# Layer 0's down projection: where the masked low-rank terms are multiplied

## The chip, the core and the metric

The kernel runs on one core of one Trainium2 chip. The core has TensorE (PE) for matrix products, VectorE (DVE), ScalarE (ACT) and GpSimd (POOL) for elementwise work, SyncE (SP) for issuing transfers, and 16 transfer (DMA) engines. PE writes its sums to PSUM, eight banks; the other operands lie in SBUF, on 128 partitions ("rows" below). The metric is device time in microseconds; the time before is the median of three runs, 1496.06 us (1492.9 to 1497.18).

## The reference, cut to what matters

Eight sequences of 128 tokens, 512 features, go through four layers. Each adds to `x` the result of an inner block followed by an outer one; everything is float32. The change touches the inner block of layer 0 only:

```python
# B = 8 sequences, H = 512, F = 1376, rank 16; an adapter per sequence
def lora_add(base, inp, A, B):
    Ab, Bb = A[0][lora_indices], B[0][lora_indices]
    t = einsum('bri,bni->bnr', Ab, inp)
    return base + einsum('bor,bnr->bno', Bb, t) * 0.5
gate = lora_add(einsum('bnh,fh->bnf', x, W_gate), x, A_gate, B_gate)
up   = lora_add(einsum('bnh,fh->bnf', x, W_up), x, A_up, B_up)
act  = silu(gate) * up
down = lora_add(einsum('bnf,hf->bnh', act, W_down), act, A_down, B_down)
```

So `down`, for each output feature and token, is a sum over 1376 hidden features plus a sum over 16 ranks of the sequence's own adapter. Layers 1 to 3 (adapters, an attention over a paged cache, experts) follow and are the same in both kernels.

## The kernel before, in words

Everything is kept transposed, features on the partitions and the 1024 tokens along the free dimension. The tokens are cut into four quarters of 256 (two sequences each); `quarter(j)` names the columns of quarter `j`, and `slot(j)` the partitions 32j to 32j+31. A half `g` is the quarters 2g and 2g+1.

**Low-rank terms.** `gathered` (L326) fetches with POOL the eight chosen adapters' rows: partition 32j+16i+r of `Bd` holds rank `r` of sequence 2j+i. So each slot has the two sequences of one quarter. `lora_down` (L574) multiplies `h` with the turned `Ad` into the PSUM tile `td`, one slot and one quarter at a time; `pair_masked` (L372) then halves it and sets to zero, in each slot, the ranks of the sequence that a token doesn't belong to. The result is `tdm`, 128 x 256: slot j, column t is for token t of quarter j.

**The hidden features.** 1376 is ten pieces of 128 and a last one of 96. `h` (128 x 11 x 1024) holds the activations; in its last piece the rows 96 to 127 are unused. The loop over pieces (`gates_by_seven`, L439) fills `h`. The weights `wd[k]` (`down_loaded`, L507) hold all 11 pieces for the output features 256k to 256k+255, loaded by SP while the gates run.

**The down projection.** `Down(g, k)` (L582) computes the 256 x 512 block of output half `k` and token half `g`, as 2 x 2 blocks of 128 x 256. The ten full pieces are cut into two halves of NH = 5 and multiplied by a Strassen-like scheme with seven block products in place of eight: `begin` does the first, `go_on` the other six. Sums of weights come from POOL (`down_weights`, L519), sums of activations from VectorE (`h_sums`, L532). At the end of `go_on` the last, 96-row piece is added to each of the four blocks by an ordinary product. Then `lora` (L621) adds the low-rank terms: for each block a product with only 32 rows, `Bd[slot(q)]` by `tdm[slot(q)]`, q the block's quarter. `out` (L626) evicts the four blocks to `y0`, one by ScalarE, three by VectorE, which also add what the scheme left in SBUF (`dp`, `du`).

**Order.** Instructions go to each engine's queue in the order in which the program lists them, and `kept` holds listed ones in place. Around the change TensorE does: the last gates (f = 10); the turning of `wb1`; `begin` of (0,0); `w11`; the turning of `Ad`; `begin` of (0,1); `td`; `go_on` of (0,0) and of (0,1); `lora` for both; (1,0) whole; the router products `midp` of half 0; (1,1) whole; `lora` for both; then layer 0's outer block (`midTp`, `eo`). SP's queue holds the gate weights, `wb1`, and behind them the loads of attention, which wait for room that the down projection frees. Several tiles share room by tag: `wb1` takes that of `Au`, the turned `Ad` that of `Bg`.

Of the kernel before, what the change touches and what calls it, by code (L numbers as in the profile page):

```python
# [10 lines left out]
F32 = mybir.dt.float32  # L11
# [6 lines left out]
P = 128  # L18
NB = 8
NT = NB * P  # L20
D = 512
DC = D // P
TG = NT // 512
FF = 1376
NF = (FF + P - 1) // P
# [22 lines left out]
def forward(ctx: ExitStack, tc: tile.TileContext, a: dict, out: bass.AP):  # L48
    nc = tc.nc
    pe, act, dve, pool, sp = nc.tensor, nc.scalar, nc.vector, nc.gpsimd, nc.sync  # L50
# [19 lines left out]
    w0 = c0.enter_context(tc.tile_pool(name="w0", bufs=1))  # L70
# [138 lines left out]
    def load_small(dst_pool, name, shape, src, tag=None, bufs=None):  # L209
        kw = {} if bufs is None else {"bufs": bufs}  # L210
        t = dst_pool.tile(shape, F32, tag=tag or name, name=name, **kw)
        sp.dma_start(t, src)
        return t
# [109 lines left out]
    with c0:  # L323
        psp = c0.enter_context(tc.tile_pool(name="psp", bufs=8, space=PSUM))

        def gathered(name, n):  # L326
            t = w0.tile([P, n], F32, tag=name, name=name)
            pool.indirect_dma_start(
                out=t, out_offset=None, in_=a[name],
                in_offset=bass.IndirectOffsetOnAxis(ap=row0_i[:, 0:1], axis=0),  # L330
            )
            return t
# [6 lines left out]
        Bg, Bu = gathered("Bg", FF), gathered("Bu", FF)  # L339
        Ad, Bd = gathered("Ad", FF), gathered("Bd", D)  # L340
# [19 lines left out]
        def quarter(j):  # L360
            return slice(j * NT // 4, (j + 1) * NT // 4)

        def slot(j):
            return slice(j * 32, (j + 1) * 32)

        def mmq(o, lhsT, rhs, start, stop):
            pe.matmul(o, lhsT, rhs, start=start, stop=stop, skip_group_check=True)  # L367

        def bank(name):
            return psp.tile([P, 2, NT // 4], F32, tag="mm", name=name)  # L370

        def pair_masked(dst, ps):  # L372

            dve.tensor_tensor(
                dst.rearrange("p (i t) -> p i t", i=2),
                ps.rearrange("p (i t) -> p i t", i=2),
                half2.unsqueeze(2).to_broadcast([P, 2, P]),
                ALU.mult,
            )
# [4 lines left out]
        tgm = w0.tile([P, NT // 4], F32, tag="tgm", name="tgm")  # L384
        tum = w0.tile([P, NT // 4], F32, tag="tum", name="tum")
# [11 lines left out]
        h = w0.tile([P, NF, NT], F32, tag="h", name="h")  # L397
# [103 lines left out]


        NH = NF // 2

        wd = []

        def down_loaded():  # L507
            for k in range(2):
                os_ = slice(2 * k * P, (2 * k + 2) * P)
                t = w0.tile([P, NF, 2 * P], F32, tag=f"wd{k}", name=f"wd_{k}")  # L510
                kept(sp.dma_start(
                    t[:, 0 : NF - 1, :],
                    a["WdT"][0 : (NF - 1) * P, os_].rearrange("(f p) o -> p f o", p=P),
                ))
                last = FF - (NF - 1) * P
                kept(sp.dma_start(t[:last, NF - 1, :], a["WdT"][(NF - 1) * P : FF, os_]))
                wd.append(t)

        def down_weights(k, t):  # L519
            w = wd[k]  # L520
            (a11, a12), (a21, a22) = (
                [w[:, NH * j : NH * (j + 1), i * P : (i + 1) * P] for j in range(2)] for i in range(2)
            )
            s1, s2, s4 = (t[:, n] for n in range(3))
            for o, l, r, op in (
                (s1, a21, a22, ALU.add), (s2, s1, a11, ALU.subtract),
                (a21, a11, a21, ALU.subtract), (s4, a12, s2, ALU.subtract),
            ):
                kept(pool.tensor_tensor(o, l, r, op))
            return a11, a12, a22, s1, s2, a21, s4  # L530

        def h_sums(g, t, held=lambda: None):  # L532
            (b11, b12), (b21, b22) = (
                [h[:, NH * i : NH * (i + 1), quarter(2 * g + j)] for j in range(2)] for i in range(2)
            )
# [6 lines left out]
        kept = tc.keep_in_program_order  # L542
# [8 lines left out]
        for f in range(1, NF):  # L551
            after = f + 1 < NF and weight_sums(f + 1, gate_weights(f + 1))
            gates_by_seven(f, A, itertools.islice(tabled, 15) if f < 3 else itertools.islice(angles, 3))
            A = after
            if f == 2:
                down_loaded()
            if f == NF // 2:
                AW = [down_weights(0, wop.tile([P, 3, NH, P], F32, tag="os", name="wds_0"))]
        cg.close()
        st = c0.enter_context(tc.tile_pool(name="st2", bufs=2, reuse_waits="tile"))  # L560


        wb1 = load_small(w0, "wb1", [P, D], a["wb1"], tag="Au")
        w11 = const.tile([P, 136], F32, tag="w11", name="w11")

        def ranks_to_ranks(wb1T):
# [5 lines left out]
        tdm = w0.tile([P, NT // 4], F32, tag="tdm", name="tdm")  # L572

        def lora_down(AdT):  # L574
            ps = bank("td")
            for f in range(NF):
                fw = min(P, FF - f * P)
                for j in range(4):
                    mmq(ps[slot(j), 0, :], AdT[:fw, f, slot(j)], h[:fw, f, quarter(j)], f == 0, f == NF - 1)
            pair_masked(tdm, ps[:, 0, :])  # L580

        class Down:  # L582

# [10 lines left out]
            def into(self, o, l, r, start=False):  # L594
                for f in range(NH):
                    mmq(o, l[:, f, :], r[:, f, :], start and f == 0, False)
# [6 lines left out]
            def go_on(self):  # L603
                a11, a12, a22, s1, s2, s3, s4 = AW[self.k]
                b11, b21, b22, t1, t2, t3, t4 = HB_[self.g]
                u, p1, even, odd = self.u, self.p1, self.even, self.odd
                self.into(odd[:, 1], s1, t1, True)
                self.into(odd[:, 0], s2, t2)
                kept(dve.tensor_tensor(u, odd[:, 0], p1, ALU.add))
                kept(dve.tensor_tensor(p1, odd[:, 1], p1, ALU.add))  # L610
                self.into(even[:, 1], s3, t3)
                kept(dve.tensor_tensor(p1, even[:, 1], p1, ALU.add))
                self.into(odd[:, 1], s4, b22)
                self.into(even[:, 0], a12, b21)
                self.into(even[:, 1], a22, t4)
                last = FF - 2 * NH * P
                for (i, j), ps in self.c.items():
                    mmq(ps, wd[self.k][:last, 2 * NH, i * P : (i + 1) * P],
                        h[:last, 2 * NH, quarter(2 * self.g + j)], False, False)

            def lora(self):  # L621
                for (i, j), ps in self.c.items():
                    o, q = 2 * self.k + i, 2 * self.g + j
                    mmq(ps, Bd[slot(q), o * P : (o + 1) * P], tdm[slot(q), :], False, True)

            def out(self):  # L626
                for (i, j), ps in self.c.items():
# [10 lines left out]
        downs = [Down(0, k) for k in range(2)]  # L638

        def meanwhile(blocks):  # L640
            HB_.append(blocks)
            wT = transposed(wb1, D, "wb1T", tag="AgT")
            downs[0].begin()
            ranks_to_ranks(wT)
            AW.append(down_weights(1, st.tile([P, 3, NH, P], F32, tag="wds", name="wds_1", bufs=1)))
            AT = transposed(Ad, FF, "AdT", tag="Bg")
            downs[1].begin()
            lora_down(AT)
# [4 lines left out]
        h_sums(1, st.tile([P, 3, NH, NT // 4], F32, tag="hs", name="hs_1", bufs=1), HB_.append)  # L653
        y0 = ypool.tile([P, DC, NT], F32, tag="y", name="y0")
        for d in downs:
            d.lora()
        for d in downs:
            d.out()
        turn_angles()
        downs = [Down(1, k) for k in range(2)]  # L660
# [4 lines left out]
        route0(0)  # L665
        downs[1].begin()
        downs[1].go_on()
        for d in downs:
            d.lora()
        for d in downs:  # L670
            d.out()

# [3 lines left out]
    with psa:  # L676
# [49 lines left out]
        kept = nc.dram_tensor("kept_x", (P, DC, NT), F32, kind="Internal").ap()  # L726
# [1607 lines left out]
```

## Time and profile before

| | |
|---|---|
| three runs: median (lowest, highest) | 1496.06 us (1492.9, 1497.18) |
| the profiled execution | 1490.35 us |
| its span, first to last instruction | 1488.6 us |
| TensorE clock granted | 0.999 of full speed |
| busy: PE, DVE, POOL, ACT | 1476.6, 1065.6, 856.4, 562.0 us |
| layer 0's down projection on the chain that ended last | 159.9 to 243.1 us, with `td` and the router |
| loads with `Bd` for `tdm`'s products | 32 records, at 201.37 and at 240.98 |

In the listings below, a row of the timeline is: start in us from the span's start, length in us, engine, line, operation, output<-inputs, rows*columns of the array (for PE), shape, count, and in brackets the idle time of that engine before it with what ended it. PEld is TensorE's loading of weights; it overlaps PE's products. A float32 product appears as two records. SPq is SP issuing a transfer.

### The profile page before, as it was taken

The numbers are of one execution on the slowest core, as the hardware profiler recorded it, in microseconds if no ns is written. First come the engines' busy times: TensorE is split into PE (matmuls) and PEld (weight loads), VectorE is DVE, ScalarE is ACT, GpSimd is POOL, SyncE is SP. The second block draws the span as 40 slices with busy tenths as digits, with TensorE's granted clock in tenths as the row PEclk, the third lists the DMA queues.
The fourth block names the chain that finished last, engine by engine and source line by source line (L and its number), as shares of the span: only waits on it lengthen the run. The fifth ranks groups of instructions, "written<-read, shape, count | busy, mean of one in ns | idle before, by whom it ended". The sixth has DMA issues, their size and how long they took to land.

```text
span 1488.6 us, 18093 instructions
## 1 busy us (share of the span) xinstructions
PE 1476.6 (99%) x5603; PEld 938.3 (63%) x5603; DVE 1065.6 (72%) x2121; ACT 562.0 (38%) x1422; POOL 856.4 (58%) x876
## 2 busy tenths in 40 slices
PE   9999999999999999999999999999999999999998
PEld 7888787455555655555555555565555555558887
DVE  4665425388888787787778778787878878855475
ACT  1111101044545544454554454454445455431110
POOL 2241104567777777776777777677777777622310
PEclk9999999999999999999999999999999999999999
DMA  7411001213545444564454455345445534433001
GB/s 242 118 44 32 1 1 55 94 36 115 183 148 173 150 119 129 150 183 126 135 152 131 128 158 177 110 135 163 129 125 166 168 106 138 120 104 98 1 9 52
DMA packets 155257, 171.44 MB, mean 115 GB/s; under 512 B 52624, under 2 KB 125776, under 8 KB 155024
## 3 DMA queue, kind: packets, MB, share of 16 engines
q1 hardware_dynamic: 136976, 133.18, 30.0%
q0 software_dynamic: 17056, 36.49, 7.7%
q8 instruction: 47, 0.77, 0.2%
q10 hardware_dynamic: 1120, 0.52, 0.1%
q14 instruction: 58, 0.48, 0.1%
HBM read 129.36 MB, written 40.76 MB: 114 GB/s over the span
## 4 chain that ended last, share of the span: by engine, by line
PE 96%; DVE 2%; ACT 0%; DMA 0%; issue 0%; DVEq 0%; ACTq 0%; SPq 0%
PE st L1173 18%; PE av L1225 18%; PE g L367 9%; PE q_six L979 8%; PE wo_two L979 6%; PE q_one L979 6%; PE q_five L979 6%; PE dn L367 5%; PE wo_six L979 4%; PE wo_one L979 4%; PE eo_l L53 3%; PE z L1761 2%; PE h L1761 2%; PE midp_l L53 1%; PE o L1761 1%; PE gu L367 1%
## 5 line engine op out<-in xcount | busy, mean ns | idle before, releaser
L922 POOL DMA_INDIRECT kn<-in_k_cache,kvrow_k x256 | 272.2, 1063 | 77.1 <-issue 71.2
L922 POOL DMA_INDIRECT vals<-in_v_cache,kvrow_v x256 | 272.3, 1064 | 73.6 <-issue 60.2
L1225 PE MATMUL av<-pT,vals 128*128 128x512 f32 x640 | 290.8, 592 | 0.2 <-DVE oT L1235 0.2
L1177 ACT ACTIVATE pT<-st,hide 128x512 f32<-128x512 f32 x256 | 175.9, 687 | 192.0 <-PE st L1173 178.8
L1173 PE MATMUL st<-qT,kT 128*128 128x512 f32 x512 | 237.4, 596 | 0.0
L1225 PEld LDWEIGHTS av<-pT,vals 128*128 128x128 f32 x640 | 121.4, 190 | 152.7 <-issue 148.3
L1078 POOL TENSOR_TENSOR vq<-q,txq 128x256 f32<-128x256 f32 x128 | 121.1, 976 | 130.6 <-ACT sqq L1052 92.9
L1173 PEld LDWEIGHTS st<-qT,kT 128*128 128x128 f32 x512 | 97.2, 191 | 109.3 <-issue 103.3
L1193 DVE TENSOR_TENSOR part<-pT 128x512 f32<-128x512 f32 x128 | 88.3, 691 | 76.2 <-ACT pT L1177 62.8
L979 PE MATMUL q_one<-q,x 128*128 128x384 f32 x256 | 93.0, 486 | 0.0
L1052 ACT ACTIVATE sqq<-q 128x128 f32<-128x128 f32 x252 | 78.2, 310 | 10.4 <-DVE q L1028 3.8
L979 PEld LDWEIGHTS q_one<-q,x 128*128 128x128 f32 x256 | 48.5, 190 | 39.8 <-issue 14.3
L979 PE MATMUL q_six<-q_s,xs_all 128*128 128x384 f32 x192 | 69.8, 486 | 0.0
L1033 ACT COPY q<-q_one 128x256 f32<-128x256 f32 x32 | 11.9, 372 | 151.9 <-PE q_one L979 133.5
L979 PE MATMUL wo_one<-o,oT 128*128 128x256 f32 x256 | 65.9, 380 | 1.1 <-ACT k L1033 0.8
L1173 PE MATMUL st<-qT,kTn 128*128 128x512 f32 x128 | 65.4, 592 | 0.0
L979 PE MATMUL wo_two<-o_s,os 128*128 128x256 f32 x256 | 60.6, 379 | 0.3 <-DVE os L938 0.3
L1177 ACT ACTIVATE pT<-st,rs 128x512 f32<-128x512 f32 x64 | 44.0, 687 | 38.5 <-PE av L1225 18.5
L979 PEld LDWEIGHTS wo_one<-o,oT 128*128 128x128 f32 x256 | 48.5, 190 | 15.0 <-issue 1.9
L436 POOL TENSOR_TENSOR ws<-wu 128x256 f32<-128x256 f32 (+1 forms) x9 | 6.4, 711 | 86.8 <-DMA wu<-in_WuT 79.8
L1209 ACT COPY rows<-rows 32x32 f32<-32x32 f32 x96 | 20.7, 216 | 92.1 <-DVE rows L1204 91.4
L367 PE MATMUL g<-xs,ws 128*128 128x256 f32 (+1 forms) x240 | 55.1, 379 | 0.0
(461 smaller groups left out, 2838.5 us busy)
## 6 DMA issues: line engine op xcount, KB each, us to landing
turned_new<-qkt SPq DMA_DIRECT2D x120, 160.0 KB
turned_cached<-kt SPq DMA_DIRECT2D x128, 128.0 KB
kT<-turned_cached SPq DMA_DIRECT2D x32, 512.0 KB
R<-sums SPq DMA_DIRECT2D x32, 512.0 KB
qT<-turned_new SPq DMA_DIRECT2D x30, 512.0 KB
q<-in_WqT SPq DMA_DIRECT2D x8, 1024.0 KB
o<-in_WoT SPq DMA_DIRECT2D x8, 1024.0 KB
kn<-in_k_cache,kvrow_k POOLq DMA_INDIRECT x256
```

Of the source, the lines that this page charges most:

```text
L53: pe.matmul(o, lhsT, rhs, start=start, stop=stop)
L367: pe.matmul(o, lhsT, rhs, start=start, stop=stop, skip_group_check=True)
L922: kept(pool.indirect_dma_start(out=d[:, c, :], out_offset=None, in_=kc if what == "k" else vc, in_offset=bass.IndirectOffsetOnAxis(ap=kvro ...
L979: kept(pe.matmul(o, l[:, c, :], r[:, c, :], start=start and c == 0, stop=c == 1, skip_group_check=True))
L1052: kept(act.activation(sq, S[n][m][:, j, i, :], AF.Square, accum_out=S[n]["ssq"][:, j, col : col + 1]))
L1078: kept(pool.tensor_tensor(to, t[:, b, :, hi : hi + 64], wx[:, b, lo : lo + 64].unsqueeze(2).to_broadcast(list(to.shape)), ALU.mult,))
L1173: kept(pe.matmul(ps, s["kT"][:, c, 4 * j : 4 * j + 4, :] if c < 4 else s["kn"][:, j], s["qT"][:, :, REP * j : REP * (j + 1), :].rearrange( ...
L1177: kept(act.activation(pT[:, c, :, :].rearrange("p i t -> p (i t)"), ps, AF.Exp, **(dict(bias=hide[:, b, c : c + 1]) if c < 4 else dict(bia ...
L1193: kept(dve.tensor_tensor(o, l, r, ALU.add))
L1209: kept(act.copy(rows[0:32, g, :], rows[32 * g : 32 * g + 32, 0, :]))
L1225: kept(pe.matmul(ps, v[:, c, :], pT[:, c, :, :].rearrange("p i t -> p (i t)"), start=c == 0, stop=c == NC - 1, skip_group_check=True,))
L1761: return pe.matmul(o, lhsT, rhs, start=start, stop=stop, skip_group_check=True)
```

## The change

The 32-row products of the low-rank terms are taken out (`lora` is gone). Instead the terms ride in the last piece's products, which have 128 rows now: the rows 96 to 127 of `h`'s last piece get `tdm`'s slot j in the columns of quarter j, by four ScalarE copies behind `pair_masked`; the weights' rows 96 to 127 get the rows of `Bd`. Since `Bd`'s rows differ from quarter to quarter, there must be four sets of last-piece weights. Quarter 0's lies in `wd` itself (`Bd`'s slot 0 is copied into it by two transfers when `wd` is loaded). Quarters 1, 2 and 3 have tiles of their own (`wl`), filled by eight transfers of SP (`last_loaded`): four bring the 96 rows of `W_down` once more from memory, four bring 32 rows of `Bd` from SBUF. Their tiles take the room of `Bu`, `tgm` and `tum`, which the last gate products are done with. The order of the other instructions on TensorE, VectorE and POOL is the same; on ScalarE the eviction of block (0,0) of `Down(1,0)` stands a few places earlier.

```diff
+        LAST = FF - (NF - 1) * P
-        wd = []
+        wd, wl = [], []
 ...
-                last = FF - (NF - 1) * P
-                kept(sp.dma_start(t[:last, NF - 1, :], a["WdT"][(NF - 1) * P : FF, os_]))
+                kept(sp.dma_start(t[:LAST, NF - 1, :], a["WdT"][(NF - 1) * P : FF, os_]))
+                kept(sp.dma_start(t[LAST:, NF - 1, :], Bd[slot(0), os_]))
                 wd.append(t)
+        def last_loaded():
+            wl.append([wd[k][:, NF - 1, :] for k in range(2)])
+            both = w0.tile([P, 2, D], F32, tag="Bu", name="wl_12")
+            ends = [w0.tile([P, 2 * P], F32, tag=t, name=f"wl_3_{t}") for t in ("tgm", "tum")]
+            wl.extend([[both[:, i, 2 * k * P : (2 * k + 2) * P] for k in range(2)] for i in range(2)])
+            wl.append(ends)
+            for t, h_ in ((both[:, 0], slice(0, D)), (both[:, 1], slice(0, D)), (ends[0], slice(0, 2 * P)), (ends[1], slice(2 * P, D))):
+                sp.dma_start(t[:LAST], a["WdT"][(NF - 1) * P : FF, h_])
+            for q, t, h_ in ((1, both[:, 0], slice(0, D)), (2, both[:, 1], slice(0, D)), (3, ends[0], slice(0, 2 * P)), (3, ends[1], slice(2 * P, D))):
+                sp.dma_start(t[LAST:], Bd[slot(q), h_])
 ...
         wb1 = load_small(w0, "wb1", [P, D], a["wb1"], tag="Au")
+        last_loaded()
 ...
             pair_masked(tdm, ps[:, 0, :])
+            for j in range(4):
+                act.copy(h[LAST:, NF - 1, quarter(j)], tdm[slot(j), :])
 ...
-                last = FF - 2 * NH * P
                 for (i, j), ps in self.c.items():
-                    mmq(ps, wd[self.k][:last, 2 * NH, i * P : (i + 1) * P],
-                        h[:last, 2 * NH, quarter(2 * self.g + j)], False, False)
-            def lora(self):
-                for (i, j), ps in self.c.items():
-                    o, q = 2 * self.k + i, 2 * self.g + j
-                    mmq(ps, Bd[slot(q), o * P : (o + 1) * P], tdm[slot(q), :], False, True)
+                    q = 2 * self.g + j
+                    mmq(ps, wl[q][self.k][:, i * P : (i + 1) * P], h[:, NF - 1, quarter(q)], False, True)
 ...
-        for d in downs:
-            d.lora()
         for d in downs:
             d.out()
```

The last removal stands twice, once for each half of the tokens.

More of the change, by code (lines that the diff above doesn't have):

```diff
@@ L667, in forward @@
         downs[1].go_on()
-        for d in downs:
-            d.lora()
         for d in downs:
```

## The prediction

> **What bounds the kernel now.** I read the page's head first: the busy shares, and the chain that ended last.
>
> ```profile
> PE 1476.6 (99%) x5603; PEld 938.3 (63%) x5603; DVE 1065.6 (72%) x2121; ACT 562.0 (38%) x1422; POOL 856.4 (58%) x876
> PE 96%; DVE 2%; ACT 0%; DMA 0%; issue 0%; DVEq 0%; ACTq 0%; SPq 0%
> ```
>
> TensorE is the bound over the whole span of 1488.6 us, and 96% of the chain is TensorE's own work. No other engine exceeds 72%. A busy PE is not proof of a bound, because a matmul's end is modelled; so I asked for the chain by pieces between 140 and 270 us, the end of layer 0's gates to the start of layer 1:
>
> ```profile
> 167.00 4.89 PE td L367 x88
> 171.89 48.62 PE dn L367 x230
> 220.51 3.71 PE midp_l L53 x32
> 224.22 18.87 PE dn L367 x94
> 243.08 0.59 PE midTp_l L288 x4
> 243.67 8.58 PE eo_l L53 x20
> ```
>
> Every piece begins where the last ends and all are PE. The down projection (`dn`) is therefore on the path that sets the end, and every PE microsecond taken out of it should move all that follows. Now the weight loads of TensorE over the two places where the diff removes products (start, length, what was loaded, count, idle before):
>
> ```profile
> 199.34 1.70 PEld L367 LDWEIGHTS dn<-h,wd 96*128 96x128 f32 x8
> 201.37 1.70 PEld L367 LDWEIGHTS dn<-tdm,Bd 32*128 32x128 f32 x16 [0.33 <-issue]
> 203.40 0.94 PEld L367 LDWEIGHTS dn<-h,wd 128*128 128x128 f32 x5 [0.33 <-PE dn L367]
> ...
> 218.40 1.70 PEld L367 LDWEIGHTS dn<-h,wd 96*128 96x128 f32 x8
> 220.13 0.99 PEld L53 LDWEIGHTS midp_l<-wmr,y 128*128 128x128 f32 x7
> ...
> 238.95 1.70 PEld L367 LDWEIGHTS dn<-h,wd 96*128 96x128 f32 x8
> 240.98 1.70 PEld L367 LDWEIGHTS dn<-tdm,Bd 32*128 32x128 f32 x16 [0.33 <-issue]
> 243.01 0.42 PEld L288 LDWEIGHTS midTp_l<-ident,mw_l 128*128 128x128 f32 x4 [0.33 <-PE dn L367]
> ```
>
> One f32 matmul shows as two records, so x16 are the eight low-rank products of one `lora` pass. The reader should see two things: each pass has a bubble of 0.33 us on either side, and at 218.40 the same 96-row piece is followed by full-array work 1.73 us after its start, with no bubble.
>
> **Removed: two passes of low-rank products.** The middle pair is the control: without a pass, the next work starts 1.73 us after the piece's start. With a pass it starts 203.40 − 199.34 = 4.06 us after it, and 243.01 − 238.95 = 4.06. Each pass costs 4.06 − 1.73 = **2.33 us** (0.33 + 1.70 + 0.33 less the usual 0.03 step), both **4.66 us**. That holds if both bubbles go. Are they waits for something else that stays? In the program the first instruction after each pass waits for TensorE's own counter alone, at 462 and at 649 before (462 and 641 after), values reached tens of matmuls earlier. So nothing is awaited there; the bubbles go with the change of the array from 128 to 32 rows and back. They were also seen around each 32-row group of the gates. If one per pass stayed, the gain would be 2 x 2.00 = 4.0; if both stayed, 2 x 1.67 = 3.35 us.
>
> A rule speaks against counting this much. The Trainium skill (TensorE: Matmul & The Clock Gate, Part 3, packing small matmuls) says that products of 32 rows in distinct row groups run concurrently, 3.07 times as fast for four. By it the sixteen records at 0.2155 us (1.70/8 = 0.213, with the step 1.73/8 = 0.216) would cost 16 x 0.2155 / 3.07 = 1.12 us, a pass 1.12 + 0.63 = 1.75 and the saving 3.5 us. The row has 1.70: each pass uses only the two slots of its own half of the tokens, so two run together, not four. I take the row.
>
> **Changed: the last piece from 96 to 128 rows.** The same 16 products (32 records), now with `wl` and `h` on 128 rows. A 96-row load takes 0.190 us like a 128-row one, and eight records take 1.70 against 2.13 for ten full ones (0.213 each way): **0**. As this change is in row count inside the full array, I bound it at ±0.1 us for all four pieces.
>
> **Added on ScalarE: four copies of `tdm` into rows 96 to 127 of `h`.** A 32x256 copy is not shown; the nearest rows are 216 ns (32x32) and 372 ns (128x256), so 0.9 to 1.5 us in all; I take 1.5. ScalarE and VectorE around it:
>
> ```profile
> 167.05 0.41 ACT L601 COPY dp_dn<-dn 128x256 f32<-128x256 f32 x1
> 202.54 0.37 ACT L630 COPY y<-dn 128x256 f32<-128x256 f32 x1 [35.07 <-PE dn L367]
> ...
> 172.01 0.43 DVE L374 TENSOR_TENSOR tdm<-td,half 128x256 f32<-128x256 f32 x1 [1.34 <-PE td L367]
> ```
>
> The copies can run from 172.44 and end by about 174. The earliest last piece starts its loads at 184.66 and needs them there, and ScalarE's next work is 28 us away: 10 us of slack, cost **0**. Without that cover it would be at most their 1.5 us.
>
> **Added on SP: ten transfers.** Two small ones (`Bd`, 32 rows) go between the loads of `wd` at 39 to 44 us, eight (`last_loaded`) behind the last gate weights. SP's queue after them:
>
> ```profile
> 132.25 0.37 SPq L80 DMA_DIRECT2D wu<-in_WuT  x1
> 243.22 0.37 SPq L898 DMA_DIRECT2D q<-in_WkT  x1
> ```
>
> SP issues nothing for 111 us, so nothing is pushed back at the second place. The eight reuse the room of `tgm`, `tum` and `Bu`, free when the last gate products end (about 159.9). Issues of `wd`'s 96-row piece took 0.69 and, behind 2.6 MB, 2.83 us; here the transfer engines stand at a share of 0.00 from 159 to 201 us, so I take 0.69: 8 x 0.69 = 5.5, all issued by 165.4. Landing: the first load of `x`, issued at 0.73, had been used at 5.18, so 4.5 us bounds one: landed by 170. The first product on `wl` (slot 1) comes at 185.5. Slack 15 us, cost **0**; even at 2.83 each, the first and second copies' six issues end at 176.9 and land by 181.4. At the first place SP's next issue waits at 50.40 for its buffer, and `wd`'s issues end at 43.74: two more at 0.69 to 2.83 end by 45.1 to 49.4, still before it. Those weights feed POOL sums at 55.08, needed at 67.39. **0**.
>
> **Added waits on TensorE.** The last pieces now wait for ScalarE and for pairs of DMA counters, with the rest of `dn` queued behind. All are past when reached. A matmul with two waits already stands at 205.45, right behind its predecessor's end at 205.42: **0**, at worst 0.05 x 5 = 0.25 us as an estimate from that 0.03 us step.
>
> **Downstream.** The results `y0` of the first half of the outputs are evicted earlier (they no longer wait for the pass); those of the second still end 1.2 to 1.6 us behind the last product. The loads of attention at 243.22, POOL's products at 243.31 and the cache gathers behind them are all released by the last `dn`, so they shift with it and no relative distance changes.
>
> **Sum.** −4.66, with edges −3.1 (bubbles stay, waits cost) and −4.8. The profiled execution took 1490.35 us around its span of 1488.6; changed: span 1483.9, execution 1485.7. The three timed runs were 1492.9, 1496.06 and 1497.18; their median lies above their mean 1495.4 and the profiled run is lower still. I centre on the mean: 1495.4 − 4.66 = **1490.7 us**. Measurement tells 0.3% (4.5 us) from no change; the change is worth 0.31% by itself, so the class is close.
>
> **Rivals.**
> Full passage (chance 0.68): 1490.7. For it: the unbroken PE chain. I give 0.54 to a reading beyond 0.3% and 0.14 to one within, the excess coming from the median's place above the mean.
> The passes were cheaper than they look (0.12): the drains stay, [...]−3.35: 1492.0 from the mean, within 0.3% mostly. Against: the control at 218.40.
> Swallowed later (0.10): attention's chain includes transfers and VectorE at about 80% busy; a shifted arrival could cost PE waits of some us: 1493 to 1497. Against: PE's idle time between 372 and 1116 us is zero.
> More is gained (0.04): earlier evictions shorten a later wait, 1488. PE's own waits are under 1.3 us each, so hardly.
> Slower (0.06): the eight transfers land late and TensorE stands in the middle of `dn`. Its place is the piece for slot 1 at 185.5. It decides once they land after 185.5 + 4.66 = 190.2, that is 30 us after their room is free; beyond 0.3% slower from 194.7, e.g. at 197: 1490.7 + 11.5 = 1502. Against it: idle transfer engines.
>
> **Range.** 1487.0 to 1496.0: above it takes in the cheaper passes and most of the swallowed case; below, 3.7 us for the spread of the runs (1490.35 to 1497.18). Faster 0.54 + 0.04 = 0.58, same 0.14 + 0.12 + 0.10 = 0.36, slower 0.06.
>
> **What the changed profile would show.** Last pieces as 128*128 with x8 loads in 1.70 us, followed after 0.03 us by `begin` of the second half and by the transposes; no 32*128 rows in `dn`; the first at about 201.07 instead of 203.40, the transposes at 238.35 instead of 243.01. `h<-tdm` on ScalarE near 172.5; eight SP issues from 159.2 to about 165. I am wrong if a bubble of over 0.1 us stands before a last piece, or if the distance from the transposes to the end (1245.6 us) grows.

## The result and the profile after

The changed kernel takes 1490.85 us (median of 16 runs, 1486.79 to 1496.33) against 1494.98 us for the kernel before (16 runs, 1492.68 to 1498.42). The ratio is 0.9973 with a 95% interval of 0.9963 to 0.9982: it is faster by 4.0 us, with the interval from 2.7 to 5.5 us. The predicted time was 1490.7 us. The profiled execution has a span of 1485.0 us, 3.6 us less than before.

The head of the page and the shares of the chain that ended last, in the changed kernel:

```profile
span 1485.0 us, 18055 instructions
PE 1471.3 (99%) x5571; PEld 934.6 (63%) x5571; DVE 1063.7 (72%) x2121; ACT 563.6 (38%) x1426; POOL 856.4 (58%) x876
PE 94%; DVE 3%; DMA 1%; issue 1%; ACT 0%; SPq 0%; DVEq 0%; ACTq 0%
```

TensorE has 32 records fewer (5571 against 5603), which are the sixteen 32-row products. It is still the bound, with 94% of the chain. Now TensorE's weight loads at the two places, in the timeline of the changed kernel:

```profile
198.84 0.84 PEld L367 LDWEIGHTS dn<-h,wd 128*128 128x128 f32 x4
199.71 0.84 PEld L367 LDWEIGHTS dn<-h,wl 128*128 128x128 f32 x4
200.57 2.13 PEld L367 LDWEIGHTS dn<-h,wd 128*128 128x128 f32 x10
202.73 4.29 PEld L367 LDWEIGHTS dn<-hs,wds 128*128 128x128 f32 x20
...
236.22 0.84 PEld L367 LDWEIGHTS dn<-h,wl 128*128 128x128 f32 x4
237.09 0.84 PEld L367 LDWEIGHTS dn<-h,wl_tum 128*128 128x128 f32 x4
237.95 0.58 PEld L288 LDWEIGHTS midTp_l<-ident,mw_l 128*128 128x128 f32 x4
238.49 0.30 PEld L53 LDWEIGHTS eo_l<-y,base 128*128 128x128 f32 x2
```

From the start of the last pieces to the work behind them it is 200.57 − 198.84 = 1.73 us and 237.95 − 236.22 = 1.73 us; both were 4.06 us before. The brackets for idle time are gone at both places, and the pieces of 128 rows (`wl` among them) step at the same 0.216 us per load as the 96-row ones did. What was added on the other engines, ScalarE first, then SP:

```profile
171.98 1.67 ACT L596 COPY h<-tdm 32x256 f32<-32x256 f32 x4 [5.00 <-DVE tdm L374]
199.26 0.37 ACT L640 COPY y<-dn 128x256 f32<-128x256 f32 x1 [25.62 <-PE dn L367]
...
40.00 0.64 SPq L517 DMA_DIRECT2D wd<-Bd  x1
43.30 0.67 SPq L517 DMA_DIRECT2D wd<-Bd  x1
49.91 0.37 SPq L80 DMA_DIRECT2D wg<-in_WgT  x1
...
161.65 1.15 SPq L530 DMA_DIRECT2D wl<-Bd  x2
163.23 0.51 SPq L530 DMA_DIRECT2D wl_tum<-Bd  x1
238.47 0.41 SPq L904 DMA_DIRECT2D q<-in_WkT  x1
```

The copies end at 173.65, and the first last piece starts at 184.17. The eight transfers are all issued by 163.74, and SP's next issue is 75 us later. One thing did not fit at first: the distance from the transposes to the end was 1245.6 us before and is 1247.05 us here. That is the mark which I had named as one that would make me wrong, so the experiments had to tell whether the change makes that loss of 1.45 us.

### The profile page after: what moved, and what is told of

Same layout as the page of the kernel before. It is cut to its first block, busy times and chain, and to the rows that moved or that the text cites. A ratio compares the mean times of both kernels' runs of the same rounds, so it can differ in the third digit from the quotient of the medians.

```text
span 1485.0 us, 18055 instructions
## 1 busy us (share of the span) xinstructions
PE 1471.3 (99%) x5571; PEld 934.6 (63%) x5571; DVE 1063.7 (72%) x2121; ACT 563.6 (38%) x1426; POOL 856.4 (58%) x876
## 4 chain that ended last, share of the span: by engine, by line
PE 94%; DVE 3%; DMA 1%; issue 1%; ACT 0%; SPq 0%; DVEq 0%; ACTq 0%
PE st L1179 18%; PE av L1231 17%; PE g L367 9%; PE q_six L985 8%; PE q_one L985 6%; PE q_five L985 6%; PE wo_two L985 5%; PE dn L367 5%; PE wo_one L985 4%; PE wo_six L985 3%; PE eo_l L53 3%; PE h L1767 2%; PE z L1767 2%; PE o L1767 1%; PE midp_l L53 1%; PE gu L367 1%
```

## The experiments

One kernel is compared with another best where single executions don't scatter. From the turning of `wb1` (the first work after the gates) to the second group of router products (`midp` of half 1, some 9 us into layer 0's outer block), TensorE's loads are so regular that two profiles of the same kernel agree within 0.01 us. I call this distance the stage; it holds the whole down projection and what follows the second pass. Its ends, in the kernel before and then in the changed one:

```profile
159.89 0.42 PEld L351 LDWEIGHTS wb1T<-ident,wb 128*128 128x128 f32 x4 [0.36 <-issue]
251.67 0.19 PEld L53 LDWEIGHTS midp_l<-wmr,y 128*128 128x128 f32 x1 [0.24 <-issue]
...
159.40 0.42 PEld L351 LDWEIGHTS wb1T<-ident,wb 128*128 128x128 f32 x4 [0.36 <-issue]
246.76 0.19 PEld L53 LDWEIGHTS midp_l<-wmr,y 128*128 128x128 f32 x1 [0.24 <-issue]
```

The table has the stage beside the start before it, the rest behind it and the time relative to the kernel before on the same chip. That matters: the kernel before has a median of 1490.0 us in 39 runs on the chip of most experiments (called chip A here), and of 1494.3 us in 7 runs on that of `before_again` and `late_14_held` (chip B), which is more than the change is worth. The chip of the first two profiles is not on record.

| kernel | turning of `wb1` | stage | rest | ratio (95%) |
|---|---|---|---|---|
| before | 159.89 | 91.78 | 1236.93 | 1 |
| before_again | 159.85 | 91.78 | 1240.97 | one run |
| after | 159.40 | 87.36 | 1238.24 | 0.9973 (0.9963 to 0.9982) |
| after_again | 163.04 | 87.35 | 1235.21 | 0.9970 (0.9958 to 0.9982) |
| no_terms | 161.11 | 87.36 | 1235.33 | 0.9973 (0.9964 to 0.9981) |
| adds_only | 160.90 | 91.77 | 1235.43 | 0.9995 (0.9987 to 1.0004) |
| first_half | 160.09 | 89.54 | 1236.07 | 0.9981 (0.9974 to 0.9988) |
| tall_pass | 160.20 | 94.28 | 1235.62 | 1.0016 (1.0007 to 1.0025) |
| interleaved | 159.57 | 91.56 | 1234.67 | one run |
| late_4 | 159.85 | 87.35 | 1235.60 | one run |
| late_14 | 160.31 | 89.67 | 1236.02 | one run |
| late_14_held | 160.48 | 101.90 | 1239.02 | 1.0070 (1.0046 to 1.0094) |

**Only the removal.** The passes are taken out of the kernel before and nothing is put in their place. This leaves the low-rank terms out of the down projection.

```diff
-                        h[:last, 2 * NH, quarter(2 * self.g + j)], False, False)
+                        h[:last, 2 * NH, quarter(2 * self.g + j)], False, True)
 ...
-        for d in downs:
-            d.lora()
```

> The kernel before without the two passes of 32-row products; the low-rank terms of the down projection are left out, and nothing is added in their place. Theory (the passes and their two bubbles were on the path, what the change adds costs nothing): TensorE's chain from the first last piece to the transposes of layer 0's mix is shorter by 4.55 us, and the time falls as with the change, by 3.5 to 5 us (ratio 0.9966 to 0.9977). Rival (the additions cost TensorE or the transfers something): this kernel is faster than the changed one by 1 us or more.

Measured: the stage is 87.36 us, equal to the changed kernel's to 0.01 us, and the ratio 0.9973 is the same. On TensorE, the terms ride in the last piece's spare rows for nothing.

**Only the additions.** All transfers and copies of the change, but the old 96-row pieces and the old passes.

```diff
 # on the changed kernel
-                    q = 2 * self.g + j
-                    mmq(ps, wl[q][self.k][:, i * P : (i + 1) * P], h[:, NF - 1, quarter(q)], False, True)
+                    mmq(ps, wd[self.k][:LAST, 2 * NH, i * P : (i + 1) * P],
+                        h[:LAST, 2 * NH, quarter(2 * self.g + j)], False, False)
 ...
+        for d in downs:
+            d.lora()
```

> All that the change adds (ten transfers, four ScalarE copies into h's spare rows) beside the old 96-row pieces and the old passes. Theory: within 0.1% of before (under 1.5 us either way), no new bubble on TensorE between 159 and 243 us. Rival (additions cost, or the shifted order of DMA counters costs attention something): slower by 1 us or more, with more waits for qT transfers in attention.

Measured: a stage of 91.77 us against 91.78, a ratio of 0.9995 whose interval includes 1. Its loads at the first place have the old shape, with both bubbles:

```profile
200.34 1.70 PEld L367 LDWEIGHTS dn<-h,wd 96*128 96x128 f32 x8
202.38 1.70 PEld L367 LDWEIGHTS dn<-tdm,Bd 32*128 32x128 f32 x16 [0.33 <-issue]
204.41 2.02 PEld L367 LDWEIGHTS dn<-h,wd 128*128 128x128 f32 x10 [0.33 <-PE dn L367]
```

So the additions by themselves cost nothing that shows (the interval ends at 0.6 us slower), and together with the run before this the gain is the removal's.

**One half.** Only the first half of the tokens uses `wl`; the second keeps its 96-row piece and its pass.

```diff
 # on the changed kernel
+                    if self.g == 0:
+                        mmq(ps, wl[q][self.k][:, i * P : (i + 1) * P], h[:, NF - 1, quarter(q)], False, True)
+                    else:
+                        mmq(ps, wd[self.k][:LAST, 2 * NH, i * P : (i + 1) * P], h[:LAST, 2 * NH, quarter(q)], False, False)
 ...                                      # second half only
+        for d in downs:
+            d.lora()
```

> The change for the first half of the tokens only; the second half keeps its 96-row pieces and its pass. Theory: half the gain, TensorE 2.3 us earlier at the transposes, time lower by 1.7 to 2.7 us. Rival (the gain comes from the second pass alone, at the border to attention, or the later kernel swallows part of it): under 1 us.

Measured: the stage is 89.54 us, 2.24 less than before, and the time is lower by 2.8 us (1.8 to 3.9), a little more than the 1.7 to 2.7 us expected. The first pass gives half of the gain by itself; the second, at another place, gives the 2.18 us that are left to the changed kernel's stage.

**Is the loss behind the stage the change's?** The changed kernel and the kernel before, once more each.

> The changed kernel once more. Theory (the 1 us that its profiled execution lost behind layer 0, mostly waits for qT transfers in attention, is jitter of single executions): these waits differ from the first profile by some us in sum, layer 0's marks do not by over 0.1 us once the first load is taken off; time 0.9973 of before within 0.001. Rival (the change causes them): the same 6 to 7 us of waits for qT again.

> The kernel before once more, for its own spread: 83.1 us from the turning of wb1 to the transposes of layer 0's mix as in its first profile (within 0.05), a start of the turning that differs by up to 3 us with the first loads, and 1243 to 1247 us from the transposes to the end.

The second profile of the changed kernel has a rest of 1235.21 us, 3.0 us less than its first, with the same stage. The second of the kernel before has 1240.97, 4.0 more than its first; from its transposes to the end it takes 1249.63 us, where I had expected 1243 to 1247. But these are not profiles of one chip. The eight of chip A have rests of 1234.67 to 1236.07 with no order by kernel: 1235.21, 1235.60 and 1236.02 with the change (`late_4` and `late_14` among them), 1235.43, 1235.62 and 1234.67 with the passes (`adds_only`, `tall_pass`, `interleaved`). The two of chip B have 1240.97 and 1239.02. So on one chip no loss of the change shows beyond a scatter of 1.4 us, and the larger differences lie between chips. The largest single wait of the first profile of the changed kernel, 2.2 us ahead of `q_six`, is also in the second profile of the kernel before; in the eight of chip A, `q_six` waits 0.5 us in all under that name. What makes it is open. The waits of TensorE's loads (in total, times, longest), changed kernel first, then the kernel before, second profile:

```profile
PEld q_six L985 <- issue: 2.7, 3, 2.2
PEld st L1179 <- DMA qT<-turned_new: 3.3, 5, 0.9
```

```profile
PEld q_six L979 <- issue: 2.8, 3, 2.3
PEld st L1173 <- DMA qT<-turned_new: 4.4, 7, 1.0
```

My expectation spoke of 6 to 7 us of waits for `qT` in the first profile; that sum had mixed waits named so with neighbours that the trace names "issue". By name they are 3.3 us there, 4.4 in the second, 7.1 in the kernel without terms: no order by kernel either. The mark of 1245.6 us was a bad one: it is a single profile's, and over all twelve the rest differs by 6.3 us, more than the whole gain. The start differs too (159.40 to 163.04): at the latest of them, TensorE had waited 2.4 us for the gathered `Au`.

**Where the bubbles come from.** The passes stay products of their own, but on 128 rows: `tdm` is spread over four tiles that are zero outside their slot.

```diff
+            tall.append(w0.tile([P, 4, NT // 4], F32, tag="Bu", name="tall"))
+            pool.memset(tall[0], 0.0)
             pair_masked(tdm, ps[:, 0, :])
+            for j in range(4):
+                act.copy(tall[0][slot(j), j, :], tdm[slot(j), :])
 ...
-                    mmq(ps, Bd[slot(q), o * P : (o + 1) * P], tdm[slot(q), :], False, True)
+                    mmq(ps, Bd[:, o * P : (o + 1) * P], tall[0][:, q, :], False, True)
```

> The kernel before with its passes kept as products of their own, but on 128 rows: tdm is spread over four 128x256 tiles with zeros outside the own slot, and multiplied by all rows of Bd. Sixteen records per pass at 0.2155 us. Theory (the bubbles come from the change between 128 and 32 rows of the array): no bubble around the passes, each 3.45 us against 2.33, so 2.2 us slower than before. Rival (the bubbles belong to a wait or a drain at the pass's place): 0.33 us on either side stay, each pass 4.1, 3.5 us slower.

```profile
199.65 1.70 PEld L367 LDWEIGHTS dn<-h,wd 96*128 96x128 f32 x8
201.38 3.43 PEld L367 LDWEIGHTS dn<-tall,Bd 128*128 128x128 f32 x16
204.83 2.13 PEld L367 LDWEIGHTS dn<-h,wd 128*128 128x128 f32 x10
```

No bubble on either side, at the same place and with the same work ahead and behind: the bubbles belong to the change of the array to 32 rows (from the 96 of the last piece) and back to 128. From 96 to 128 rows there is none. The time is higher by 2.4 us (1.0 to 3.7), and the stage by 2.50. The stage says more than the 2.24 which I had worked out, and that shows a small error of the prediction (below).

**What packing gives.** The kernel before, with the slots of a pass taken in turn.

```diff
-                for (i, j), ps in self.c.items():
+                for (i, j), ps in sorted(self.c.items(), key=lambda at: at[0]):
                     o, q = 2 * self.k + i, 2 * self.g + j
```

> The kernel before with the products of each pass in the order first slot, second slot, first, second, in place of first, first, second, second. Theory (two slots run together, so sixteen records take half of sixteen full ones): the pass stays within 0.1 us of 1.70. Rival (what the packing rule would have for distinct row groups side by side): nearer to 1.1 to 1.4 us.

```profile
199.01 1.70 PEld L367 LDWEIGHTS dn<-h,wd 96*128 96x128 f32 x8
201.05 1.59 PEld L367 LDWEIGHTS dn<-tdm,Bd 32*128 32x128 f32 x16 [0.33 <-issue]
202.97 2.02 PEld L367 LDWEIGHTS dn<-h,wd 128*128 128x128 f32 x10 [0.33 <-issue]
```

The pass takes 1.59 us for 1.70, just beyond the 0.1 us that I had allowed. With 0.2155 us for a full record, sixteen are 3.45 us, so two slots run 2.0 times (2.2 in turn) as fast as full ones. In the kernel before, the gates have 32-row products of the same 256 columns that take all four slots in turn:

```profile
145.51 0.31 PEld L367 LDWEIGHTS g<-tgm,Bg 32*128 32x128 f32 x8 [0.33 <-issue]
145.83 0.42 PEld L367 LDWEIGHTS g<-tum,Bu 32*128 32x128 f32 x8
146.58 0.68 PEld L367 LDWEIGHTS g<-x,wg 128*96 128x96 f32 x4 [0.33 <-issue]
```

Sixteen records take 0.74 us there (145.51 to 146.25), against 1.59 with two slots in turn. So the number of slots counts. The Trainium skill's 3.07 (TensorE: Matmul & The Clock Gate, Part 3) is for four row groups; a pass has two and doesn't reach it. A pass over four slots in the down projection was not tried.

**What a late transfer costs.** Ahead of the eight transfers, quarter 1's weights are loaded 4 or 14 times more, each load waiting for the one before.

```diff
+            for _ in range(4):      # 14 in the second
+                sp.dma_start(both[:LAST, 0], a["WdT"][(NF - 1) * P : FF, :])
```

> The changed kernel with four more copies of the 96 rows of W_down loaded one after another into quarter 1's weights, each waiting for the one before, ahead of the eight transfers. Theory (about 15 us of slack): the last transfer is issued some 8 to 12 us later, at about 175, and no bubble stands before a last piece. Rival (slack nearly gone): TensorE idles before the piece for slot 1 at 185.

With four, the last transfer is issued at 171.62 (8 us later) and the stage is 87.35 us: no effect, as the slack says.

> As the run with four, with fourteen copies. Theory: the chain of loads takes some 30 us or more, quarter 1's weights land at about 195, TensorE idles before that piece by some 10 us, and the whole kernel is that much longer, about 6 us slower than before. Rival (the piece is off the path, or the wait is caught up later): under 2 us slower than the changed kernel.

With fourteen, the last one is issued at 197.12 and the stage is longer than the changed kernel's by only 2.3 us. Neither side of the expectation came true, and for a reason outside of the chip: when the kernel was built, the planner that lists the instructions had moved the two products of slot 1 behind 52 other loads.

```profile
185.95 4.29 PEld L367 LDWEIGHTS dn<-hs,wds 128*128 128x128 f32 x20
...
196.74 0.41 PEld L367 LDWEIGHTS dn<-hs,wd 128*128 128x128 f32 x2
199.59 0.73 PEld L367 LDWEIGHTS dn<-h,wl 128*128 128x128 f32 x4 [2.45 <-issue]
```

From 185.95 to 197.15 TensorE does other work, and only 2.45 us of waiting are left. So the text ahead of the prediction says too much where it says that the queues follow the program's listing; instructions not held by `kept` can be moved. I held the order of the down projection's products to that of the changed kernel:

```diff
-                    mmq(o, l[:, f, :], r[:, f, :], start and f == 0, False)
+                    kept(mmq(o, l[:, f, :], r[:, f, :], start and f == 0, False))
 ...                                      # the last pieces likewise
```

> As the run with fourteen extra copies, but TensorE's order held to that of the changed kernel, so that slot 1's product stays in the middle of the down projection (in the run with fourteen the planner had moved it 14 us back at build time, and the stall was only 2.45 us). Theory of the slower rival: quarter 1's weights land at about 199.5, TensorE idles from about 186 to 199.5, the down projection is some 13 us longer than in the changed kernel, and the time is 8 to 10 us above before. Rival (later work catches up what a stall loses): under 5 us above before.

SP's chain of loads and TensorE around the piece, and then some stretches (from and to, length, busy time of PE, PEld, DVE, ACT and POOL, granted clock, transfer share, GB/s):

```profile
166.86 27.02 SPq L528 DMA_DIRECT2D wl<-in_WdT  x12
195.97 0.31 SPq L530 DMA_DIRECT2D wl<-in_WdT  x1
...
185.24 0.84 PEld L367 LDWEIGHTS dn<-h,wd 128*128 128x128 f32 x4
198.51 1.35 PEld L367 LDWEIGHTS dn<-h,wl 128*128 128x128 f32 x4 [12.43 <-issue]
199.96 5.85 PEld L367 LDWEIGHTS dn<-hs,wds 128*128 128x128 f32 x20
...
186.00:188.00 2.00, 0.48 (x3) 0.08 (x1) 0.00 (x0) 0.00 (x0) 0.00 (x0) 1.00 0.19 63
188.00:190.00 2.00, 0.00 (x0) 0.00 (x0) 0.00 (x0) 0.00 (x0) 0.00 (x0) 0.86 0.14 49
190.00:192.00 2.00, 0.00 (x0) 0.00 (x0) 0.00 (x0) 0.00 (x0) 0.00 (x0) 0.50 0.25 84
...
202.00:203.00 1.00, 1.00 (x4) 0.73 (x3) 0.00 (x0) 0.00 (x0) 0.00 (x0) 0.50 0.00 0
203.00:204.00 1.00, 1.00 (x6) 0.90 (x5) 0.00 (x0) 0.00 (x0) 0.00 (x0) 0.95 0.00 0
```

TensorE idles 12.43 us, and nothing later catches it up: the stage is 14.5 us longer than the changed kernel's (13 expected), and the time 1.0070 of before, 10.5 us more (6.9 to 14.0; 8 to 10 expected). The slower rival's mechanism is real; the changed kernel is just far from it. Twelve loads take 195.97 − 166.86 = 29.1 us, or 2.4 us from the issue of one (96 x 2 KB) to that of the next. By that, slot 1's last rows in the changed kernel, issued by 162.8, land at about 165 (an estimate); the profile agrees, as its transfer engines move nothing from 164.75 to 168. That is some 20 us ahead of their use at 185.03.

## Why the prediction was right, point by point

The third point rests on the work that follows each pass in the kernel before:

```profile
203.40 2.02 PEld L367 LDWEIGHTS dn<-h,wd 128*128 128x128 f32 x10 [0.33 <-PE dn L367]
205.45 4.29 PEld L367 LDWEIGHTS dn<-hs,wds 128*128 128x128 f32 x20
...
243.01 0.42 PEld L288 LDWEIGHTS midTp_l<-ident,mw_l 128*128 128x128 f32 x4 [0.33 <-PE dn L367]
243.40 0.30 PEld L53 LDWEIGHTS eo_l<-y,base 128*128 128x128 f32 x2
```

- **The number.** That 1490.7 us lies so near the measured 1490.85 is in part luck: the start was taken 0.4 us too high (1495.4 for 1494.98) and the gain 0.5 us too large (4.66 for 4.13, the difference of the medians), and the two cancel.
- **The path.** TensorE's unbroken chain through the down projection was read rightly. What the stage loses, the time loses: 4.4 us in the stage, 4.0 (2.7 to 5.5) in the time; 2.2 and 2.8 (1.8 to 3.9) for one half.
- **The size of the removal.** The step 4.06 to 1.73 us came at both places exactly. Yet the stage is shorter by 91.78 − 87.36 = 4.42 us, not 4.66. The term that was mis-sized is the bubble behind each pass: work that follows it runs in faster. `begin` behind the pass took 203.40 to 205.45, 2.05 us; behind the last piece it takes 200.57 to 202.73, 2.16. The transposes took 0.39 us from start to start, now 0.54. That gives back 0.11 + 0.15 = 0.26 us (0.24 by the stage), and also accounts for the 128-row passes' 2.50 in place of 2.24 us.
- **The bubbles' cause.** Put down to the change of the array's rows, because no wait stood there: shown by the passes on 128 rows, which have no bubble.
- **The rule of packing.** Taking the row (1.70) over the estimate from the skill's factor (1.12) was right: 3.5 us would have been foretold, 4.42 were seen. That two slots, not four, set the row was argued from the program; the gates' groups bear it out.
- **96 to 128 rows.** No cost: 1.73 us for the piece either way.
- **Copies and transfers.** Free, as the run with only the additions shows. The four copies took 1.67 us where I took at most 1.5 from the nearest row; inside 10 us of slack it doesn't matter. The slack of the transfers was underrated (20 us, not 15): slot 1's rows were issued by 162.8 and not 165.4, and 4.5 us was a loose bound for a landing.
- **The slower rival.** Its price was one microsecond per microsecond of lateness. Its place and its sign hold; the price is higher (14.5 us for 12.4 us of waiting), because the granted clock halves during the stall. At build time the planner may dodge it.
- **The classes.** Here I was too sure. I gave 0.58 to more than 0.3%; the ratio is 0.27%, with 0.3% inside its interval. The step that failed is the centring: three runs of before had a high median, and from it I took an excess beyond the change's own 0.31%. With 16 runs on each side no excess is left; and the change's own worth was 4.42 / 1494.98 = 0.30%, on the line itself. What came is the branch of the full passage to which I had given 0.14.

## What to carry to other kernels

Where a contraction has a last piece with empty rows, look whether a small low-rank product fits into them. Here it cost nothing on TensorE: the piece took 1.73 us with 96 rows and with 128, while a separate pass on 32 rows took 1.70 us and a bubble of 0.33 us each way. Measure such an edit on a stage whose length doesn't scatter, from one fixed instruction to another, and compare times on one chip only; 39 executions of the kernel before on one chip ran from 1487.07 to 1493.95 us, more than the whole gain apart. And see what the new operands' slack is by making them late on purpose, with the order of the instructions held.

## What the runs showed of the hardware that I had not expected

A bubble of 0.33 us at a change of array rows is not its whole account: the work that follows starts up 0.11 to 0.15 us sooner than it does behind the last piece. That is not the bubble's alone. In the changed kernel the ten loads of a `begin` take 2.05 us from start to start behind the transposes of `wb1` (159.79 to 161.84) and 2.06 behind the router's products (221.21 to 223.27), without a bubble, and 2.16 behind the last piece. What sets it is open.

A stall costs more than its length. In the held run the granted clock was 1.00 up to 188, 0.50 from 190 on, and 0.50 still until 203, though TensorE worked again from 198.51. The four `wl` loads took 1.45 us from start to start in place of 0.87, the twenty behind them 5.87 in place of 4.31: together the 2.1 us by which the stage's 14.54 us exceed the wait. The wait of 2.45 us in the run with fourteen left the clock at 1.00. The Trainium skill (TensorE: Matmul & The Clock Gate, Part 1) says that TensorE falls to half its clock after about 3.4 us of idling. The rows agree in the half, and so do the two waits, 2.45 us without a fall and 12.43 us with one; what lies between was not tried. No wait of TensorE's loads in the changed kernel's profile is longer than 2.2 us.
